# A convolution block stack on one core: softmax and norms spread over calendar ticks, block loads on GpSimd's queue, an inner product between two others

## The chip, the cores and the metric

The kernel runs on one core of a Trainium2 chip. The metric is the time of one execution in microseconds (us); lower is better. Three executions of the kernel before took 2953.84, 2951.65 and 2955.03 us. One more execution was taken with the hardware profiler; all profile lines here are from it.

## What is computed

The input x has 32 images of 14 x 14 positions and 512 channels, in float32. Two layers follow, each added to its input:

```python
x = x + L0(_gn(x))          # 18 blocks of gelu(x @ w[i] + b[i])
x = x + grouped_conv3x3(_gn(x), W)   # 32 groups

def L0(x):
    anchors = []
    for i in range(18):
        nx = gelu(x @ block_w[i] + block_b[i])
        if i in (11, 14, 17):                       # targets
            h = gelu(mean(nx, (1, 2)) @ fc1_w[t] + fc1_b[t])
            gates = softmax((h @ fc2_w[t] + fc2_b[t]).reshape(-1, 3, 512), axis=1)
            nx = nx + gammas[t] * sum_a(gates[:, a] * anchors[a])
        x = nx
        if i in (1, 4, 9):
            anchors.append(x)
    return x
```

`_gn` is a group norm over 32 groups of 16 channels without weights.

## The kernel before

**Tiles and pairs.** Two images (392 positions) make a tile, two tiles a pair; there are eight pairs, 0 to 7. Channels lie on the partitions. One *block* is one layer i of one pair p, written (p,i) here: a 512x512 weight matrix times 784 columns. The list `steps` gives the order of the blocks: pair 0's layers 0 to 11, and then, for each p, the first twelve layers of pair p+1 woven with the last six of pair p, three at a time. The blocks are numbered 0 to 144 in this order; block 141 is a gap that only carries other work.

**A block** (`block`, L538) multiplies 2x2 partitioned matrices with seven products in place of eight, with sums of weights (`s`, stored once in DRAM as `skeep`) and differences of activations (`t`). One of the seven is split once more in the same way (`Inner`, L495); its four parts are 128x196 matmuls between the 128x392 matmuls of the others, with weights `u` (kept in `ukeep`) and right sides `v`. PSUM accumulators are called x, y and z, two banks each. The first product, x, is copied by ScalarE to y (`save`, L599); the second product then adds to y, and a gelu (L576, for target layers L583) makes the first quarter of the output. The last quarter's gelu comes near the end of the block; the next block's y needs it.

A block *starts ahead* when `ahead(k)` (L387) is true: its first product is then an inner product whose parts were already run inside the block before. It is false for pair 0, for layer 0, for layers right behind a target and for (6,16): 40 blocks of 144. These begin with x (written at L613), the copies to y, then y (L617), then `inner.part(0)` of z.

**The calendar.** All other work is put on ticks, seven to a block, and `run(tick)` calls what stands there at seven places of the block's text. Ticks only fix the order in which instructions are written to the engines' queues; each engine then runs its queue in order and waits where it must. `ROOM` says how many us VectorE ("dve") and ScalarE ("act") have free in each tick of a block, and `put` (L130) takes the first tick with room. VectorE's room is 2.1, 0.8, 2.2, 2.6, 0.5, 0, 0 for ticks 0 to 6.

**The work that the change touches.**

- `plan_start` (L357) brings in a pair while an earlier one is computed. `copy_in` (L263) copies x to the DRAM tensor `xcol`. `load_blocks` (L270) loads one of eight parts: four DMAs `xb` of 32 partitions x 12 x 32 floats (48 KB in pieces of 128 bytes), and for every second part four DMAs `xr` of 8 KB. They go to SyncE's (SP's) queue, which also issues the weights (L404 to L409), `s` (L427) and `u` (L450). Three buffers take the parts; `turn_blocks` (L284) transposes one on VectorE in 32x32 squares, and the part three places on is loaded into its buffer. Then come statistics, `scales_mean` and `scales_rstd` (group sums on TensorE, small VectorE operations, a power on GpSimd), `scales_newton` and `norm_in`.
- Behind a target layer, `plan_head` (L841) puts `gate_hidden` (L717) and `gate_logits` (L733, TensorE) and `gate_softmax` (L743) on ticks of the following blocks. `gate_softmax` is VectorE, then ScalarE's tanh (L763), then VectorE again. `plan_gates` then puts `gate_part` (VectorE), `gate_last` (ScalarE, tile gq) and `gate_add`.
- The functions with `yield` are written so that each engine's share is a step; `whole` runs all steps at once, in one tick.
- GpSimd's (POOL's) queue holds the powers and 32 accumulating DMAs of `keep_base` (L784), `o<-xkeep`.

Behind the last block, `drain` lists the remaining tasks in an order of its own. The change leaves it alone.

Of the kernel before, what the change touches and what calls it, by code (L numbers as in the profile page):

```python
# [20 lines left out]
def kernel(  # L21
# [20 lines left out]
    nc = tc.nc  # L42
# [4 lines left out]
    NH = NCK // 2  # L47
    NI = 2
    N = NI * HW
    NT = B // NI  # L50
    NPAIR = NT // 2
# [36 lines left out]
    def whole(parts):  # L88

        for _ in parts:  # L90
            pass
# [8 lines left out]
    for p in range(NPAIR - 1):  # L100
        q = p + 1
        if q < NPAIR - 1:
            parts = [(q, 0, 3), (p, 12, 15), (q, 3, 6), (p, 15, 18), (q, 6, 12)]
# [17 lines left out]
    def at(tick, fn, *args):  # L121
        calendar[tick].append((fn, args))

    def room(e, tick):
        return left[e].get(tick, ROOM[e][tick % NP7] if tick < tend else TAIL[e])

    def hold(e, tick, us):
        left[e][tick] = room(e, tick) - us

    def put(first, need, fn, *args):  # L130

        tick = first
        while any(room(e, tick) < us for e, us in need.items()):
            tick += 1
        for e, us in need.items():
            left[e][tick] = room(e, tick) - us
        at(tick, fn, *args)
        return tick

    def run(tick):  # L140
        for fn, args in calendar.pop(tick, ()):
            fn(*args)


    ident = const.tile([P, P], F32, name="ident")
    make_identity(nc, ident)
# [67 lines left out]
    def scales_mean(d, lo=0, hi=NR):  # L214
        ps = group_sums(f"mps_{d['name']}_{lo}", d["st"][:, lo:hi, 1::3], hi - lo)
        yield
        st, mean, dv = d["st"][:, lo:hi], d["mr"][:, 0, lo:hi], d["dv"][:, lo:hi]
        nc.vector.tensor_scalar(mean, ps, 0.5, None, ALU.mult)
        nc.vector.tensor_tensor(
            dv, st[:, :, 1::3], mean.unsqueeze(2).to_broadcast([P, hi - lo, 2]), ALU.subtract  # L220
        )
        nc.vector.tensor_mul(dv, dv, dv)
        nc.vector.scalar_tensor_tensor(dv, dv, HW / 2.0, st[:, :, 2::3], ALU.mult, ALU.add)

    def scales_rstd(d, lo=0, hi=NR):

        ps = group_sums(f"vps_{d['name']}_{lo}", d["dv"][:, lo:hi], hi - lo)
        yield
        ve = d["ve"][:, lo:hi]
        nc.vector.tensor_scalar(ve, ps, 1.0 / HW, 1e-5, ALU.mult, ALU.add)  # L230
        yield
        nc.gpsimd.tensor_tensor(d["y"][:, lo:hi], ve, mhalf[:, lo:hi], ALU.pow)
# [10 lines left out]
    def scales_newton(d, lo=0, hi=NR, times=1):  # L243
        ve, y, e, mr = d["ve"][:, lo:hi], d["y"][:, lo:hi], d["e"][:, lo:hi], d["mr"]
        for i in range(times):
            nc.vector.tensor_mul(e, y, y)
            nc.vector.scalar_tensor_tensor(e, e, -0.5, ve, ALU.mult, ALU.mult)
            o = y if i < times - 1 else mr[:, 1, lo:hi]
            nc.vector.scalar_tensor_tensor(o, e, 1.5, y, ALU.add, ALU.mult)
        nc.vector.scalar_tensor_tensor(  # L250
            mr[:, 2, lo:hi], mr[:, 0, lo:hi], -1.0, mr[:, 1, lo:hi], ALU.mult, ALU.mult
        )
# [5 lines left out]
    TB = 32  # L258
# [11 lines left out]
    def load_blocks(t, c):  # L270
        d = starts.setdefault(t, {"xin": {}})
        cols = xcol[t // 2][t % 2 * N : (t % 2 + 1) * N].rearrange("n (k q i) -> q n k i", k=NCK, i=TB)
        xs = d["xin"][c] = inpool.tile([P, NTB, TB], F32, tag="xin", name=f"xb_{t}_{c}")
        for q in range(P // TB):
            nc.sync.dma_start(
                xs[q * TB : (q + 1) * TB],
                cols[q, : NTB * TB, c].rearrange("(n j) i -> j n i", j=TB),
            )
        if c % NH == 0:
            xr = d["xr", c // NH] = inpool.tile([P, NH, TB], F32, tag="xr", name=f"xr_{t}_{c}", bufs=2)  # L280
            for q in range(P // TB):
                nc.sync.dma_start(xr[q * TB : (q + 1) * TB], cols[q, N - TB :, c : c + NH])

    def turn_blocks(t, c):  # L284
        d = starts[t]
# [16 lines left out]
    pst = {}  # L302
# [54 lines left out]
    def plan_start(p):  # L357

        t0 = NP7 * at_step[p, 0]
        parts = [(2 * p + n, c) for n in range(2) for c in range(NCK)]  # L360
        NIN = 3
        a = t0 - LEAD
        at(a - 30, copy_in, p)
        turned = []
        b = 0
        for j, (t, c) in enumerate(parts):
            at(t0 - LEAD - 6 if j < NIN else turned[j - NIN], load_blocks, t, c)
            turned.append(put(max(a, turned[j - NIN] + 4 if j >= NIN else 0), {"dve": 0.45 + c % NH * 0.15}, turn_blocks, t, c))
            a = turned[j]
        for j, (t, c) in enumerate(parts):  # L370
            b = max(b, put(turned[j // NH * NH + NH - 1], {"dve": 0.7}, stats_in, t, c))
        b = put(b + 1, {"dve": 0.8}, lambda: whole(scales_mean(pst[p])))
        b = put(b + 1, {"dve": 0.2}, lambda: whole(scales_rstd(pst[p])))
        b = put(b + 2, {"dve": 0.8}, lambda: scales_newton(pst[p]))
        e = b
        for c in range(NCK):
            for n in range(2):
                e = max(e, put(b, {"dve": 0.8}, norm_in, p, c, (n,)))
        b = e

        assert b < t0 - 2
        at(t0 - 3, take_start, p)
# [4 lines left out]
    def ahead(k):  # L387


        p, i = steps[k]  # L390
        if (p, i) == (NPAIR - 2, TARGETS[1] + 2):
            return False
        return p > 0 and i not in (GAP, 0) and i - 1 not in TARGETS
# [144 lines left out]
    def block(k):  # L538
# [17 lines left out]
        def part(acc, d, lhsT, rhs, first=False, kks=range(NH)):  # L556
            for kk in kks:
                nc.tensor.matmul(  # L558
                    acc[d][:, :N], lhsT=lhsT[:, kk, d * P : (d + 1) * P],
                    rhs=rhs[:, kk, :], start=first and kk == 0, stop=kk == NH - 1,  # L560
                    skip_group_check=True,
                )
# [5 lines left out]
        def gelu(half, n, srcs, ds=range(NH)):  # L568
            if 0 in ds:
                dst[half][n] = quarter(f"o{half}{n}_{name}")  # L570
            o = dst[half][n]
            for d in ds:
                c = half * NH + d
                r = i * NCK + c
                if pooled is None:
                    nc.scalar.activation(  # L576
                        o[:, d, :], srcs[d], AF.Gelu_apprx_tanh, bias=bias[:, r : r + 1]
                    )
                else:
                    for b in range(NI):  # L580
                        sl = slice(b * HW, (b + 1) * HW)
                        m = n * NI + b
                        nc.scalar.activation(  # L583
                            o[:, d, sl], srcs[d][:, sl], AF.Gelu_apprx_tanh,
                            bias=bias[:, r : r + 1], accum_out=pooled[:, c, m : m + 1],
                        )
# [4 lines left out]
        def flat(acc):  # L591
            return [b[:, :N] for b in acc]
# [17 lines left out]
        else:  # L610
            X, Y = bank("x"), bank("y")
            for d in range(NH):
                part(X, d, w["a11"], q[0][0], True)  # L613
                save(Y, X, (d,))
        for kk in range(NH):
            for d in range(NH):
                part(Y, d, w["a12"], q[1][0], kks=(kk,))  # L617
        gelu(0, 0, flat(Y))
        Z = bank("z")
        inner = Inner(Z, s[0], w["u0"], t[0], t["v"], f"z{name}")  # L620
        inner.part(0)
        run(tick)
        c2 = temps(2)
        part(X, 0, s[1], t[1])
# [216 lines left out]
    def plan_head(p, i):  # L841

        k = at_step[p, i]
        t1 = NP7 * (k + 1)
        name = f"{p}_{i}"
        ti = TARGETS.index(i)
        box = boxes[p, i] = {}
        hn = [(h, n) for h in range(2) for n in range(2)]
        if i == NB - 1:
            for h, n in hn:  # L850
                a = max(boxes[p, TARGETS[-2]]["base"].values()) + 1
                assert put(a, {"act": 1.0}, keep_base, p, h, n) < t1 - NP7
        if k == len(steps) - 1:
            for (h, n), a in (((0, 0), 2), ((1, 1), 5), ((0, 1), 6)):
                at(NP7 * k + a, gate_base, p, i, h, n)
            return
        if p == 0:
            at(t1 + 1, gate_differences, k, ti)
        at(t1 + 1, lambda: whole(gate_hidden(k, ti, name, box)))
        box["base"] = {(h, n): put(t1, {"dve": 1.0}, gate_base, p, i, h, n) for h, n in hn}  # L860
        a = t1 + 2
        while room("dve", a) < 1.75:
            a += 1
        at(a, gate_logits, k, name, box)
        return put(a, {"dve": 1.75}, lambda: whole(gate_softmax(ti, name, box)))

    def plan_gates(p, t, a, chunks):

# [617 lines left out]


    NGAP = 6
    LEAD = 47
    for k in range(len(steps)):  # L1490
        p, i = steps[k]
        if i == GAP:
# [41 lines left out]
    b = NP7  # L1534
# [46 lines left out]
```

## Time and profile before

| | |
|---|---|
| median of three executions | 2953.84 us |
| profiled execution, its own time | 2947.32 us |
| its span, first to last instruction | 2945.6 us |
| TensorE (PE) busy | 2864.8 us, 97% |
| VectorE (DVE) busy | 2116.1 us, 72% |
| ScalarE (ACT) busy | 1630.1 us, 55% |
| GpSimd (POOL) busy | 79.1 us, 3% |
| DMA, mean | 172 GB/s |
| granted TensorE clock | 0.993 |

In the profile's lines, a group or a timeline row gives engine, line of the kernel, operation, output<-inputs with buffer numbers left out, and shapes. In a timeline row the first number is the start and the second the length, both in us, and the bracket at the end says how long the engine stood idle before it and who ended that. A float32 matmul shows as two records, so a product of four matmuls is "x8". "SPq" is the issuing of DMAs by SyncE; its length is the time of issue, not of the transfer. A line of the waits view reads: who waited <- for whom: us in total, times, longest. A busy TensorE is not a TensorE at its peak, since the ends of its pipelined matmuls are modelled.

### The profile page before, as it was taken

Reading aid. Unit: us, or ns where it says so; the run is one execution under the profiler, and the core shown is the slowest. Engines: PE = TensorE matmul, PEld = TensorE weight load, DVE = VectorE, ACT = ScalarE, POOL = GpSimd, SP = SyncE. Lnnn points to the kernel's source line nnn. Section 1 sums busy time; section 2 is a strip of 40 time slices with the busy share of each in tenths; the row PEclk is TensorE's granted clock in tenths of the full one; section 3 lists DMA queues with packets and bytes.
Section 4 is the critical chain, followed back from the end, with each engine's and each line's share of the span. In section 5 each row is a group of like instructions: output and inputs, shape, how many; then the busy total and the mean of one; then the engine's idle time right before and its main releaser. Section 6 shows DMA issues by size and latency. Waiting matters only on the chain.

```text
span 2945.6 us, 36255 instructions
## 1 busy us (share of the span) xinstructions
PE 2864.8 (97%) x11169; PEld 1960.5 (67%) x11169; DVE 2116.1 (72%) x4576; ACT 1630.1 (55%) x4281; POOL 79.1 (3%) x59
## 2 busy tenths in 40 slices
PE   9999999999999999999999999999999999999977
PEld 5666666666666666667666666666766676666666
DVE  6888887877778565875768756687567865766765
ACT  4445555566555665655556555565555555655551
POOL 0000000000000000000000000000000000000000
PEclk9999999999999999999999999999999999999999
DMA  6644566646564566647566465654766655453676
GB/s 205 180 163 158 172 191 174 183 139 195 163 183 143 162 185 172 187 135 209 170 188 187 142 185 168 189 165 148 203 177 184 175 151 155 143 161 125 180 212 160
DMA packets 528882, 505.69 MB, mean 172 GB/s; under 512 B 246883, under 2 KB 370610, under 8 KB 528690
## 3 DMA queue, kind: packets, MB, share of 16 engines
q1 hardware_dynamic: 513194, 485.30, 55.1%
q0 software_dynamic: 4608, 12.85, 2.5%
q10 hardware_dynamic: 10888, 5.22, 0.7%
q8 instruction: 91, 1.49, 0.2%
q14 instruction: 101, 0.83, 0.1%
HBM read 415.56 MB, written 98.93 MB: 175 GB/s over the span
## 4 chain that ended last, share of the span: by engine, by line
PE 84%; DVE 5%; ACT 5%; DMA 3%; SPq 1%; issue 1%; POOL 0%; ACTq 0%; DVEq 0%; POOLq 0%
PE x L558 36%; PE y L558 13%; PE z L507 11%; PE z L558 11%; PE x L507 7%; PE cps L1099 4%; ACT o L576 2%; PE lps L738 1%; ACT y L599 1%; DVE c L603 1%; ACT gq L823 1%; DMA x<-x2d 1%; PE hps L721 1%; DMA w<-ukeep 1%; DMA s<-skeep 1%
## 5 line engine op out<-in xcount | busy, mean ns | idle before, releaser
L558 PE MATMUL x<-t,s 128*128 128x392 f32 x2304 | 856.8, 494 | 5.0 <-DMA s<-skeep 2.9
L558 PEld LDWEIGHTS x<-t,s 128*128 128x128 f32 x2304 | 422.5, 190 | 167.3 <-DVE v_x L473 3.6
L558 PE MATMUL y<-o,w 128*128 128x392 f32 x1088 | 391.5, 500 | 23.3 <-ACT o L576 20.2
L558 PE MATMUL x<-t,w 128*128 128x392 f32 x1152 | 403.0, 492 | 0.0
L558 PE MATMUL z<-o,s 128*128 128x392 f32 x1088 | 398.0, 494 | 0.0
L603 DVE TENSOR_TENSOR c<-x,c 128x392 f32<-128x392 f32 x288 | 163.1, 566 | 277.6 <-ACT c L599 256.7
L576 ACT ACTIVATE o<-c,bias 128x392 f32<-128x392 f32 x480 | 282.9, 618 | 135.2 <-DVE c L603 134.6
L558 PEld LDWEIGHTS y<-o,w 128*128 128x128 f32 x1088 | 200.0, 189 | 201.4 <-ACT o L576 61.1
L599 ACT COPY c<-x 128x392 f32<-128x392 f32 x288 | 139.8, 485 | 323.5 <-PE x L558 323.5
L558 PEld LDWEIGHTS x<-t,w 128*128 128x128 f32 x1152 | 216.2, 190 | 130.8
L603 DVE TENSOR_TENSOR c<-z,c 128x392 f32<-128x392 f32 x288 | 157.8, 561 | 163.9 <-PE z L558 163.9
L491 DVE TENSOR_TENSOR t<-o,o 128x784 f32<-128x784 f32 x272 | 263.6, 969 | 6.5 <-ACT o L576 6.5
L558 PEld LDWEIGHTS z<-o,s 128*128 128x128 f32 x1088 | 200.8, 190 | 97.1 <-ACT c L599 0.5
L491 DVE TENSOR_TENSOR t<-o,t 128x784 f32<-128x784 f32 x272 | 263.1, 967 | 0.0
L576 ACT ACTIVATE o<-y,bias 128x392 f32<-128x392 f32 x240 | 140.8, 587 | 145.5 <-PE y L558 137.0
L507 PE MATMUL z<-v,u 128*128 128x196 f32 x864 | 214.0, 329 | 1.0 <-PE y L558 0.9
L507 PE MATMUL x<-v_x,w 128*128 128x196 f32 x832 | 193.7, 335 | 9.6 <-DMA w<-ukeep 8.9
L507 PEld LDWEIGHTS z<-v,u 128*128 128x128 f32 x864 | 156.9, 190 | 42.1 <-PE y L558 1.5
L532 DVE TENSOR_TENSOR z<-z,v 128x392 f32<-128x392 f32 x144 | 82.2, 570 | 139.3 <-ACT z L528 139.1
L507 PEld LDWEIGHTS x<-v_x,w 128*128 128x128 f32 x832 | 141.7, 190 | 48.1 <-issue 9.8
L576 ACT ACTIVATE o<-x,bias 128x392 f32<-128x392 f32 x240 | 135.5, 582 | 38.0 <-PE x L558 37.5
L599 ACT COPY y<-x 128x392 f32<-128x392 f32 x288 | 126.2, 461 | 54.1 <-PE x L558 54.0
(152 smaller groups left out, 3951.9 us busy)
## 6 DMA issues: line engine op xcount, KB each, us to landing
s<-skeep SPq DMA_DIRECT2D x504, 256.0 KB
w<-in_L_conv_block_w_dram SPq DMA_DIRECT2D x126, 512.0 KB
w<-in_L_conv_block_w_dram SPq DMA_DIRECT2D x126, 256.0 KB
u<-ukeep SPq DMA_DIRECT2D x126, 256.0 KB
w<-ukeep SPq DMA_DIRECT2D x104, 256.0 KB
x2d<-xc SPq DMA_DIRECT2D x116, 224.0 KB
x<-x2d SPq DMA_DIRECT2D x104, 224.0 KB
w<-in_L_conv_block_w_dram SPq DMA_DIRECT2D x18, 1024.0 KB
```

Of the source, the lines that this page charges most:

```text
L491: nc.vector.tensor_tensor(t[j], i0, i1, ALU.subtract)
L507: nc.tensor.matmul(self.corner(d, n), lhsT=lhsT, rhs=rhs, start=first, stop=True, skip_group_check=True,)
L532: nc.vector.tensor_tensor(both, both, self.f.unsqueeze(1).to_broadcast([P, 2, HW]), ALU.add)
L558: nc.tensor.matmul(acc[d][:, :N], lhsT=lhsT[:, kk, d * P : (d + 1) * P], rhs=rhs[:, kk, :], start=first and kk == 0, stop=kk == NH - 1, sk ...
L576: nc.scalar.activation(o[:, d, :], srcs[d], AF.Gelu_apprx_tanh, bias=bias[:, r : r + 1])
L599: nc.scalar.copy(cs[d][:, :N], acc[d][:, :N])
L603: nc.vector.tensor_tensor(cs[d], acc[d][:, :N], cs[d], ALU.add)
L721: nc.tensor.matmul(hps[:, :NB4], lhsT=w1[:, kk, :], rhs=box["pooled"][:, kk, :], start=(kk == 0), stop=(kk == NCK - 1),)
L738: nc.tensor.matmul(lps[:, m * NB4 : (m + 1) * NB4], lhsT=w2[:, (m - NCK) * P : (m - NCK + 1) * P], rhs=h, start=True, stop=True,)
L823: nc.scalar.activation(q[:, d, sl], anc[p][NA - 1][h][n][:, d, sl], AF.Identity, scale=gt[:, NA - 2, j : j + 1],)
L1099: nc.tensor.matmul(pv[:, :, lo:hi], lhsT=bw[:, g, dy], rhs=xv[:, :, lo + dy - 1 : hi + dy - 1], start=g == 0 and j == 0, stop=j == 2, skip ...
```

## The change

Four edits. (1) In a block that does not start ahead, `inner.part(0)` of z is written between the first product and y's; y's matmuls then go bank by bank. (2) `apart` runs the steps of a function on ticks of their own. The softmax of pairs 1 to 5 takes three ticks b, b+1, b+2, with b behind the tick of the logits and 1.5 us of room at b+2. (3) The input norm's two group sums take their steps on separate ticks. (4) `load_blocks` issues on GpSimd's queue, 336 DMAs in all. `LEAD` goes from 47 to 50, so a pair's load begins three ticks earlier.

```diff
+    def apart(fn, *ticks):
+        parts = []
+        def go():
+            if not parts:
+                parts.append(fn())
+            next(parts[0], None)
+        for tick in ticks:
+            at(tick, go)
...
-            nc.sync.dma_start(
+            nc.gpsimd.dma_start(
                 xs[q * TB : (q + 1) * TB],
                 cols[q, : NTB * TB, c].rearrange("(n j) i -> j n i", j=TB),
             )
...
-                nc.sync.dma_start(xr[q * TB : (q + 1) * TB], cols[q, N - TB :, c : c + NH])
+                nc.gpsimd.dma_start(xr[q * TB : (q + 1) * TB], cols[q, N - TB :, c : c + NH])
...
-        b = put(b + 1, {"dve": 0.8}, lambda: whole(scales_mean(pst[p])))
-        b = put(b + 1, {"dve": 0.2}, lambda: whole(scales_rstd(pst[p])))
-        b = put(b + 2, {"dve": 0.8}, lambda: scales_newton(pst[p]))
+        b += 1
+        e = put(b + 1, {"dve": 0.8}, lambda: None)
+        apart(lambda: scales_mean(pst[p]), b, e)
+        apart(lambda: scales_rstd(pst[p]), e + 1, e + 2, e + 2)
+        b = put(e + 4, {"dve": 0.8}, lambda: scales_newton(pst[p]))
...
-        for kk in range(NH):
-            for d in range(NH):
-                part(Y, d, w["a12"], q[1][0], kks=(kk,))
-        gelu(0, 0, flat(Y))
+        if ahead(k):
+            for kk in range(NH):
+                for d in range(NH):
+                    part(Y, d, w["a12"], q[1][0], kks=(kk,))
+            gelu(0, 0, flat(Y))
         Z = bank("z")
         inner = Inner(Z, s[0], w["u0"], t[0], t["v"], f"z{name}")
         inner.part(0)
+        if not ahead(k):
+            product(Y, w["a12"], q[1][0])
+            gelu(0, 0, flat(Y))
         run(tick)
...
-        return put(a, {"dve": 1.75}, lambda: whole(gate_softmax(ti, name, box)))
+        if p in (0, NPAIR - 2, NPAIR - 1):
+            return put(a, {"dve": 1.75}, lambda: whole(gate_softmax(ti, name, box)))
+        b = a + 1
+        while room("dve", b + 2) < 1.5:
+            b += 1
+        hold("dve", b, 0.7)
+        hold("dve", b + 2, 1.5)
+        apart(lambda: gate_softmax(ti, name, box), b, b + 1, b + 2)
+        return b + 2
...
-    LEAD = 47
+    LEAD = 50
```

## The prediction

> **What bounds the kernel.** The page's first part says that TensorE is busy for nearly the whole span, so only its waits can be won.
>
> ```profile
> PE 2864.8 (97%) x11169; PEld 1960.5 (67%) x11169; DVE 2116.1 (72%) x4576; ACT 1630.1 (55%) x4281; POOL 79.1 (3%) x59
> ```
>
> The second view is the list of who waited for whom, PE alone (us in total, times, longest):
>
> ```profile
> PE y L558 <- ACT o L576: 20.2, 41, 1.2
> ...
> PE x L507 <- DMA w<-ukeep: 8.9, 5, 2.7
> ...
> PE y L558 <- ACT y L599: 3.0, 8, 1.5
> PE x L558 <- DMA s<-skeep: 2.9, 3, 1.4
> ```
>
> These sums leave out what hides in the pipeline, so I took start-to-start spacings of the matmul records from the trace: 329 ns behind a 128x392, 166 ns behind a 128x196 when nothing waits; the excess is wait. That gives 134 us, of which start and drain hold some 46 and the change barely touches them. The rest: 45.5 us ahead of y (12.5 in the 40 blocks that do not start ahead, 33.0 in the 104 that do), about 20 for weights that came late, the rest small. Blocks that wait for nothing are 17.85 us apart.
>
> The third view is the timeline of the second block of pair 0:
>
> ```profile
> 37.97 2.80 PE L558 MATMUL x<-o,w 128*128 128x392 f32 x8
> ...
> 39.48 0.47 ACT L599 COPY y<-x 128x392 f32<-128x392 f32 x1 [0.73 <-PE x L558]
> ...
> 40.60 3.02 PE L558 MATMUL y<-o,w 128*128 128x392 f32 x8
> 40.85 0.47 ACT L599 COPY y<-x 128x392 f32<-128x392 f32 x1 [0.90 <-PE x L558]
> ...
> 43.46 0.49 PE L507 MATMUL z<-v,u 128*128 128x196 f32 x2
> ```
>
> y's second bank is copied until 41.32, while TensorE wants it two matmuls (0.66 us) after 40.60: y takes 2.86 us to the next start instead of 2.63, 0.22 lost.
>
> The fourth is the timeline around a gate's softmax, pair 2's in block (3,0):
>
> ```profile
> 941.16 1.84 PE L738 MATMUL lps<-h,w 128*128 128x4 f32 x16
> ...
> 943.05 0.19 DVE L749 TENSOR_TENSOR lg<-lps,bias 128x32 f32<-128x32 f32 x1 [1.72 <-PE lps L738]
> ...
> 945.48 0.25 DVE L774 SCALAR_TENSOR_TENSOR g<-ex,gam,ssum 128x32 f32<-128x32 f32 x1
> ...
> 946.82 1.03 DVE L603 TENSOR_TENSOR c<-z,c 128x392 f32<-128x392 f32 x2
> ...
> 948.45 0.79 ACT L823 ACTIVATE gq<-o,g 128x196 f32<-128x196 f32 x2
> ...
> 949.94 1.05 ACT L576 ACTIVATE o<-x,bias 128x392 f32<-128x392 f32 x2
> ...
> 950.57 2.90 PE L558 MATMUL y<-o,w 128*128 128x392 f32 x8 [1.20 <-ACT o L576]
> ```
>
> VectorE stands 1.72 us for the logits of its own tick, works on the softmax to 945.7, ScalarE then puts gq before the last gelu, and the next y is late.
>
> The fifth is SP's queue near 450 us:
>
> ```profile
> 446.30 2.04 SPq L275 DMA_DIRECT2D xb<-xcol  x4
> 448.38 2.08 SPq L282 DMA_DIRECT2D xr<-xcol  x4
> 450.51 4.79 SPq L275 DMA_DIRECT2D xb<-xcol  x8
> ...
> 459.56 0.59 SPq L408 DMA_DIRECT2D w<-ukeep  x1
> ```
>
> Eleven us of block loads stand ahead of the weights; a second batch follows at 461.83.
>
> **The change, part by part.**
>
> *Inner part between the products* (40 blocks not started ahead). No instruction is added. Two 128x196 matmuls (four records, 0.66 us) go between x and y, which covers the 0.22 us wait; v's last add ended at 40.16, before x ends at 40.60, so the new first operand is there. On ScalarE two Z copies (0.31 + 0.33) now precede the gelu of y, which waits for y anyway (idle 1.68 before it). Of the 12.5 us, block (6,16) alone has 1.77, where ScalarE is full of gq; it keeps 1.1. Gain 11.4. If v were late the cover would be gone and the 0.22 would stay.
>
> *Softmax on three ticks* (pairs 1 to 5, three gates each; pairs 0, 6 and 7 keep it whole). In the changed order the logits stay at tick 3, VectorE's first part goes to tick 5, tanh to tick 6, the rest to tick 0 of the next block, and gq leaves tick 4. The five waits like the one above (1.47 each by spacing, after blocks (q,0), q = 2 to 6) and the ten after (q,3) and (q,6) (0.75 each) are 7.35 + 7.5. I take 14.5. The first part (0.64 us) now precedes three 0.97 us adds; the first of them had 2.2 us to spare, so that is free; without this cover it is 15 times 0.64. Next late is the block behind, whose y waits 0.56 for a gq at tick 4 that is still there.
>
> *Norms on ticks of their own.* PE never waited for a group sum of pairs 1 to 7's input norms; VectorE stood 8.0 us for eight (mr_a from mps_a), off the path. I put 0; a gain is excluded by PE's list, a loss needs pair 1's last norm (now tick 79, pair 1 starts at 84) late. The power on POOL (2.9 us) is due 18 ticks after the last loads, so queueing behind them costs nothing.
>
> *Block loads to POOL's queue.* 224 xb (384 pieces of 128 B each) and 112 xr (64 pieces) leave SP. The six places where they stand ahead of weights and skeep loads (blocks 23, 41, 59, 77, 95, 113 and those behind) hold 18.2 us of excess. In four of these the order now has eight output stores (7.11 us of SP in block 77); stores without block loads behind blocks 68, 70 and 106 gave no wait. I take 15.5.
>
> The Trainium skill, "DMA: Bandwidth & Descriptors", section "Issuing engines are not separate DMA queues", says that issuing from another engine saves only the sequencer's time, usually small beside the transfer. By it this gain would be near 0. The rows above speak against it here: the weights were issued 8 us late because of issue alone.
>
> What POOL pays is not in the trace. The nearest row is the accumulating load, 128 pieces:
>
> ```profile
> L788 POOL DMA_DIRECT2D o<-xkeep x32: 844/874/1047, 372.9 to 2769.4; - x32
> ...
> 2175.01 1.73 POOL L788 DMA_DIRECT2D o<-xkeep  x2 [3.06 <-ACT o L787]
> ```
>
> Back to back they take 0.84 us. One xb costs c: at least 0.84 (all fixed), 2.5 if all goes by pieces (3 times 0.84), 3.1 if also stretched as the longest row is (1047 over 844). I take 1.7, the middle of the first two, since SP's own rows (xb 0.47 median for 384 pieces, xkeep 0.38 for 128) hardly grow with pieces; xr 0.7.
>
> Where it matters: the first three blocks of a pair wait on POOL only for the copy of x and the base loads, which end some 40 us before their turn (410 against 451). The next three wait for buffers that the first turns free, and the last of them lands 11c + 4 x 0.7 + 3 us later (landing 3, an estimate below the 4.7 of 392 KB). VectorE turns them 19.3 us later in pair 1 (one block of 18.6 and a turn of 0.57), 27.7 us later in pairs 3 to 7 (ten ticks). Behind a late turn on VectorE stand the c adds and pre-adds, so TensorE stops after about 2 us of slack (VectorE's idle 1.72 and 2.14 there). At c = 1.7 the sum is 24.5: pair 1 loses 3, the others 0. At 0.84 nothing is lost; at 2.5, 12 + 2.4 (pair 1's last group, 7c) + 5 x 3.6 = 32; at 3.1, 19 + 7 + 5 x 10 = 76.
>
> **Sum.** -11.4 - 14.5 - 15.5 + 3 = -38.4 us. Against the profiled execution's 2947.32 (span 2945.6) that is 2909; against the median 2953.84, which lies 6.5 above that execution, 2915. The median is the forecast.
>
> **Rivals.**
>
> *Issue on POOL between 2.1 and 2.6 us.* 8 to 40 us come back as stalls at the second turns. For it: POOL's only row is for fewer pieces. Against: SP's rows. About 2935 in the middle.
>
> *SP was not the cause.* The late weights stem from full DMA engines: four skeep loads took 7.70 us of issue at 711 us with no block loads near. Then the 15.5 is nothing and the result 2931. This is what the skill's rule above would give.
>
> *ScalarE's work only moves.* No gq is removed; y waits elsewhere. Only 4 of the 14.5 are won: 2926.
>
> *Slower: the block loads hold VectorE.* Place: second turns of pairs 1 and 3 to 7. From c = 2.6 the stalls (41 us) eat the gains; at 3.1 the result is 2953.84 - 41.4 + 76 = 2988. For it: the 1047 ns issue ran beside small VectorE operations. Against: the nine back-to-back issues are all 0.84 beside two-input VectorE adds. The Trainium skill, "SBUF — State Buffer", section "SBUF: two separate sides", has a box by which VectorE's two-port operations keep GpSimd from writing descriptors; it names 620 ns growing to 3100. The trace agrees only in that issues never fell below 844.
>
> That a part does nothing is the norms, counted as 0.
>
> **Chances.** Forecast as summed 0.56 (2905 to 2926); POOL at 2.1 to 2.6, 0.16, of which 0.05 lies within 0.2%; SP not the cause 0.10; work only moves 0.10; slower 0.08. 0.2% (5.9 us) is about what a measurement can tell from no change. Faster 0.87, same 0.05, slower 0.08. The low end takes all of 12.5, 14.85 and 18.2 with no stall (2908), less the 3 us by which the runs shown scatter: 2905; the high end reaches into POOL's case and leaves out its dear part and the slower one: 2938.
>
> **What would show it.** Right: y's 0.22 gone from pair 0 (pitch near 18.13); y after (q,0), (q,3), (q,6) without wait for pairs 1 to 5; no w<-ukeep or s<-skeep waits in blocks 23 to 114; POOL's xb at 1.7 us or less and no idle of VectorE ahead of L305's transposes. Wrong: transposes waiting for xb, or y waits as before with another releaser.

## The result

The changed kernel takes 2922.24 us (median of four executions, 2916.88 to 2926.05) where the kernel before takes 2952.74 on the same chip. The ratio is 0.9894, 95% interval 0.9874 to 0.9915: 30.5 us less. The forecast was 38.4 less, 2915, with a range of 2905 to 2938. The profiled execution took 2918.94 us (span 2916.6, against 2945.6 before).

The page's engines and its count of DMA packets:

```profile
PE 2855.6 (98%) x11169; PEld 1968.9 (68%) x11169; DVE 2115.2 (73%) x4576; ACT 1632.9 (56%) x4281; POOL 276.3 (9%) x395
...
DMA packets 441073, 505.67 MB, mean 173 GB/s; under 512 B 153699, under 2 KB 279218, under 8 KB 440882
```

No engine has other work than before but POOL, whose 79 us became 276 for 336 more instructions. The packets fell by 87,800 (528,882 before).

The list of who waited for whom, PE:

```profile
PE y L572 <- ACT o L590: 8.7, 26, 0.5
PE x L521 <- DMA w<-ukeep: 4.3, 5, 1.5
PE z L521 <- issue: 3.7, 1, 3.7
...
PE vps_b L221 <- DVE dv_b L235: 2.1, 7, 1.0
...
PE z L521 <- DVE u L473: 1.4, 1, 1.4
...
PE y L572 <- ACT y L613: 0.8, 1, 0.8
```

y's wait for the gelu fell from 20.2 to 8.7 us, y's wait for its copy from 3.0 to 0.8. The other lines tell of the costs: two waits of z that were not there (3.7 and 1.4), a group sum that waits for VectorE (2.1, from 0.3), and weights from ukeep that are still late, 4.3 in place of 8.9.

The excess of the start-to-start spacings, the measure of the prediction, fell from 132 (the prediction's count gave 134) to 103.5 us in these two profiled executions (A: blocks that start ahead, N: the others):

| place of the excess (us) | before | after |
|---|---|---|
| y, A | 33.0 | 17.5 |
| y, N | 12.5 | 2.8 |
| z's 128x196, N | 1.5 | 6.2 |
| other products; late weights are about 20 of it before, 6 after | 38.0 | 25.1 |
| output norm's sum, ahead of the drain | 0 | 2.9 |
| start and drain | 47.1 | 49.0 |

The timeline of pair 0's third block shows the new order:

```profile
60.15 0.47 ACT L613 COPY y<-x 128x392 f32<-128x392 f32 x1 [0.65 <-PE x L572]
...
60.31 0.36 DVE L487 TENSOR_TENSOR v<-v,t 128x196 f32<-128x196 f32 x1
...
60.43 0.57 PE L521 MATMUL z<-v,u 128*128 128x196 f32 x2 [0.37 <-DVE v L487]
...
61.16 2.80 PE L572 MATMUL y<-o,w 128*128 128x392 f32 x8
```

The cover works: y's second bank is copied until 60.62, before y begins at 61.16. Most blocks of pair 0, 18.35 us apart before, are now 18.12 apart, where the prediction had said 18.13. But v is not always there. Here z waits 0.37 us for it, because VectorE made four sums of weights (L473) first.

The timeline of the softmax behind block (2,0), where y had waited 1.47:

```profile
601.91 2.80 PE L572 MATMUL y<-o,w 128*128 128x392 f32 x8
...
602.66 0.17 DVE L767 TENSOR_TENSOR lg<-lps,bias 128x32 f32<-128x32 f32 x1
```

VectorE no longer waits for the logits, whose matmuls ended 7 us ago (at 595.7), and y has no bracket.

The worst place of z is block 142, (7,15), which stands behind the gap:

```profile
2739.23 2.80 PE L572 MATMUL x<-o,w 128*128 128x392 f32 x8
...
2740.05 2.76 DVE L815 TENSOR_TENSOR o<-o,o 128x784 f32<-128x784 f32 x3
...
2744.24 1.00 DVE L505 TENSOR_TENSOR t<-o,o 128x784 f32<-128x784 f32 x1
2745.28 0.36 DVE L487 TENSOR_TENSOR v<-t 128x196 f32<-128x196 f32 x1
...
2745.74 0.57 PE L521 MATMUL z<-v,u 128*128 128x196 f32 x2 [3.72 <-issue]
...
2746.48 4.49 PE L572 MATMUL y<-o,w 128*128 128x392 f32 x8
```

VectorE is still at the gap's work, starts the block's first t 5 us after x has begun, and z stands 3.7 us for v. The bracket says "issue"; the v row above it says who was late. Behind the wait, y takes 4.49 us in place of 2.80: its matmuls start 0.65 us apart, not 0.33, while the trace's granted clock is 0.5 (2746.5 to 2749.9). So y loses 1.7 us more without a bracket.

POOL's price, from the group of L287:

```profile
L287 POOL DMA_DIRECT2D xb<-xcol x224: 615/615/967, 46.3 to 2224.0; - x112
```

615 ns for a load of 384 pieces, under the 844 that the prediction had as its lowest case. No transpose of VectorE waits for an xb.

### The profile page after: what moved, and what is told of

It is laid out like the page before. It is cut to its first block, busy times and chain, and to the rows that moved or that the text cites. A ratio compares the mean times of both kernels' runs of the same rounds, so it can differ in the third digit from the quotient of the medians.

```text
span 2916.6 us, 36340 instructions
## 1 busy us (share of the span) xinstructions
PE 2855.6 (98%) x11169; PEld 1968.9 (68%) x11169; DVE 2115.2 (73%) x4576; ACT 1632.9 (56%) x4281; POOL 276.3 (9%) x395
## 3 DMA queue, kind: packets, MB, share of 16 engines
q8 instruction: 90, 1.47, 0.2%
## 4 chain that ended last, share of the span: by engine, by line
PE 88%; DVE 3%; ACT 3%; DMA 3%; SPq 1%; issue 1%; POOL 0%; DVEq 0%; ACTq 0%; POOLq 0%
PE x L572 38%; PE y L572 13%; PE z L572 12%; PE z L521 11%; PE x L521 8%; PE cps L1125 4%; PE lps L756 1%; ACT o L590 1%; DMA w<-ukeep 1%; DMA x<-x2d 1%; DVE c L617 1%; ACT gq L841 1%; ACT y L613 1%; PE hps L739 1%; DMA w<-in_L_conv_block_w_dram 0%
## 5 line engine op out<-in xcount | busy, mean ns | idle before, releaser
L572 PE MATMUL y<-o,w 128*128 128x392 f32 x1088 | 385.4, 497 | 9.8 <-ACT o L590 8.7
L287 POOL DMA_DIRECT2D xb<-xcol x224 | 138.6, 634 | 401.0 <-DVE xt L305 254.8
L806 POOL DMA_DIRECT2D o<-xkeep x32 | 28.0, 879 | 1510.8 <-ACT o L805 805.1
```

Source lines behind the costliest of these rows:

```text
L287: nc.gpsimd.dma_start(xs[q * TB : (q + 1) * TB], cols[q, : NTB * TB, c].rearrange("(n j) i -> j n i", j=TB),)
L572: nc.tensor.matmul(acc[d][:, :N], lhsT=lhsT[:, kk, d * P : (d + 1) * P], rhs=rhs[:, kk, :], start=first and kk == 0, stop=kk == NH - 1, sk ...
```

## Experiments

The theory after this result: the softmax and the loads gave what was forecast; the inner part gave only 5 us, since its cover goes where v is late; and two things that had no price took something back: the place of copy_in (moved by LEAD) and that of the output norm. Rivals: the sums of the trace are chance of one execution; late weights have nothing to do with issue; and POOL's second turns were never in danger.

### One part taken back

Four kernels, each the changed one with one part as before, on one chip (the kernel before there: 2951.34).

**The product y ahead of z again, in all blocks.**

```diff
-        if ahead(k):
-            for kk in range(NH):
-                for d in range(NH):
-                    part(Y, d, w["a12"], q[1][0], kks=(kk,))
-            gelu(0, 0, flat(Y))
+        for kk in range(NH):
+            for d in range(NH):
+                part(Y, d, w["a12"], q[1][0], kks=(kk,))
+        gelu(0, 0, flat(Y))
...
-        if not ahead(k):
-            product(Y, w["a12"], q[1][0])
-            gelu(0, 0, flat(Y))
```

> The changed kernel with the order x, y, inner part in every block, as before. By the prediction's size of this edit the time is 11.4 us above the changed kernel (2922), 2934. By the profile after, the edit won 10.9 us in the ordinary blocks but lost 5.9 in blocks 0, 2 and 142, where the inner part's operands come late: then the time is only 5 us above, 2927, the 0.22 us waits of y are back in some 38 blocks, and block 142 has its 3.95 + 1.69 us back to 1.2 + 0.2.

Measured: 2924.14, ratio 0.9914 (0.99 to 0.9929), an interval that overlaps the changed kernel's. By spacing, y in N blocks has 12.15 again and z's 128x196 there 1.52 in place of 6.2: the edit is worth 4.7 us of wait, 9.3 of y less 4.7 of z. The medians are 2 us apart, so the time alone does not show a gain. From before to after, the same two rows of the table give 5.0: the ordinary blocks and (6,16) won 10.6, nearly what was forecast, and blocks 142, 0 and 2 lost 5.6.

**The block loads on SP again.**

```diff
-            nc.gpsimd.dma_start(
+            nc.sync.dma_start(
                 xs[q * TB : (q + 1) * TB],
...
-                nc.gpsimd.dma_start(xr[q * TB : (q + 1) * TB], cols[q, N - TB :, c : c + NH])
+                nc.sync.dma_start(xr[q * TB : (q + 1) * TB], cols[q, N - TB :, c : c + NH])
```

> The changed kernel with the block loads on SyncE's queue again. If SyncE's issue time made the weights late: 14 us above the changed kernel, 2936, with waits for w<-ukeep and s<-skeep of 2 to 5 us back in five or six of the blocks 23 to 114. If the DMA engines' load was the cause and issuing from another engine saves little: no difference, 2922, and no such waits beyond those of the changed kernel.

Measured: 2930.91, 0.993 (0.9917 to 0.9943), 9 to 11 us over the changed kernel, where 14 was expected. By spacing, waits are back in blocks 78 (6.4 us), 97 (1.6) and 59 (0.5), and block 114 has 7.5 in place of 1.5. Blocks 23, 24, 41, 42, 95 and 96 still have none. So with the loads on SP, other parts of the change suffice there; the likely one is that the loads stand three ticks earlier, but no run sets LEAD back alone.

**The softmax whole again, in one tick.**

```diff
-        if p in (0, NPAIR - 2, NPAIR - 1):
+        if True:
```

> The changed kernel with the softmax of all pairs in one tick. If its waits on VectorE make y late: about 15 us above the changed kernel, 2937, with 1.47 us ahead of y behind blocks (q,0) and 0.75 behind (q,3) and (q,6) for q = 2 to 6. If ScalarE's gq work sets it and only moves: 4 us above, 2926.

Measured: 2929.68, 0.9927 (0.9914 to 0.9939). The y excess of A blocks goes from 17.5 to 28.8, with 0.75 in each of blocks (q,1), (q,4) and (q,7), q = 2 to 6. So the softmax's ticks are worth 11.3 us of y, fifteen times 0.75; by the ratios the time is 10 us longer. The output norm's wait also rises, from 2.9 to 6.9, and the weights of blocks 37 and 55 are on time, as the longer blocks would let them be.

The 1.47 that was expected in blocks (q,1) did not come back. In the kernel before, the output norm's `scales_newton` stood in the same place of block (3,0), behind the softmax and ahead of the c adds:

```profile
946.10 0.17 DVE L246 TENSOR_TENSOR e_b<-y_b 128x16 f32<-128x16 f32 x1
...
946.72 0.17 DVE L250 SCALAR_TENSOR_TENSOR mr_b<-mr_b 128x16 f32<-128x16 f32 x1
```

Its four operations take 0.79 us there. In the changed kernel, and in this one, the output norm's plan has moved and they come earlier, in the first third or so of the block. Blocks (2,1) to (7,1) each won the other 0.72 by that, 4.3 us in all; in (7,1), whose softmax stays whole in every kernel, it is seen alone (1.47 to 0.75). With the block loads alone on POOL it stays 1.47. The move is there with each single part taken back, so LEAD, or two of the other parts, made it.

**The input norm's sums whole again.**

```diff
-        apart(lambda: scales_mean(pst[p]), b, e)
-        apart(lambda: scales_rstd(pst[p]), e + 1, e + 2, e + 2)
-        b = put(e + 4, {"dve": 0.8}, lambda: scales_newton(pst[p]))
+        b = put(b + 1, {"dve": 0.8}, lambda: whole(scales_mean(pst[p])))
+        b = put(b + 1, {"dve": 0.2}, lambda: whole(scales_rstd(pst[p])))
+        b = put(b + 2, {"dve": 0.8}, lambda: scales_newton(pst[p]))
```

> The changed kernel with the input norm's group sums in one tick each, as before. By the prediction this part is worth 0: 2922 within 2 us. A rival: the freed room of VectorE moved the output norm to ticks 5 and 6, where TensorE waits for it (vps_b 3.8 us in the profile after, 0.5 before); with the norms whole these waits go and the time is 3 us lower, 2919.

Measured: 2920.05, 0.9897 (0.9883 to 0.991). No difference in the time, as forecast. By spacing two waits are gone with it, 1.1 us each in blocks 29 (the output norm's sum) and 34 (below), but late weights are more in this execution and hide that.

### The block loads alone, on the kernel before

```diff
     def load_blocks(t, c):
...
-            nc.sync.dma_start(
+            nc.gpsimd.dma_start(
                 xs[q * TB : (q + 1) * TB],
...
-                nc.sync.dma_start(xr[q * TB : (q + 1) * TB], cols[q, N - TB :, c : c + NH])
+                nc.gpsimd.dma_start(xr[q * TB : (q + 1) * TB], cols[q, N - TB :, c : c + NH])
```

> The kernel before with the block loads on GpSimd's queue and nothing else changed. By the prediction -15.5 us, and no stall since the issue costs 0.6 us: a ratio of 0.995 (14.8 us). Waits of blocks 23/24, 41/42, 59/60, 77/78, 95/96 and 113/114 (18 us of spacing) go. Rival (the rule that moving issue between queues saves little): within 3 us of the kernel before. Taking the loads back to SP in the changed kernel cost about 10 us; if that is what they are worth everywhere, it is -10 here.

Measured: 2931.04, 0.9925 (0.9908 to 0.9943), 20 us less than the 2950.98 of before; 16.4 by spacing. PE's waits for weights from ukeep, five for 8.9 us before, are one in its list, and those for skeep are gone:

```profile
PE x L507 <- DMA w<-ukeep: 1.6, 1, 1.6
```

The 18.2 us of excess in blocks 23/24, 41/42, 59/60, 77/78, 95/96 and 113/114 are all gone. That the weights stood behind the batch in SP's queue, and not in full DMA engines, can be seen in the kernel before itself. The DMA view of the 35 us from 440 us, in 40 slices of 0.875 us, busy tenths of the 16 engines:

```profile
DMA  0000007996611466624139989989997564116679
```

The first batch of block loads was issued from 446.3 to 457.2. From 448 us on (the tenth to the twenty-first digit) the DMA engines were busy for only 1 to 6 tenths. The weights w<-ukeep could have gone at about 452, as they did at 452.44 with the loads on POOL; they went at 459.56. On POOL's queue the loads also become other packets: in the trace's DMA records each piece of 128 bytes is a packet of its own on SP's queue (93,184 of them), and on POOL's 24 pieces of an xb go as one of 3072 bytes. Whether SP's batch was slow by its issues or by its packets wasn't tried apart.

The Trainium skill, "DMA: Bandwidth & Descriptors", section "Issuing engines are not separate DMA queues", has it that another issuing engine saves only the sequencer's time, usually small beside the transfer. That the gain is small does not hold here: the 336 DMAs are worth 10 us (loads back) to 20 (loads alone), and their issues took SP 185 us in the kernel before, 11 of them ahead of this block's weights.

### POOL made dear

Where is the point at which the block loads would hold VectorE? Each xb cut into four; in a second kernel the 4 is an 8.

```diff
-            nc.gpsimd.dma_start(
-                xs[q * TB : (q + 1) * TB],
-                cols[q, : NTB * TB, c].rearrange("(n j) i -> j n i", j=TB),
-            )
+            for r in range(4):
+                lo, hi = r * TB // 4, (r + 1) * TB // 4
+                nc.gpsimd.dma_start(
+                    xs[q * TB + lo : q * TB + hi],
+                    cols[q, : NTB * TB, c].rearrange("(n j) i -> j n i", j=TB)[lo:hi],
+                )
```

> The changed kernel with each xb load cut into four of 96 pieces. If an issue has a fixed part of some 0.55 us (xr, 64 pieces, takes 0.53), the load of a part of 32 columns costs GpSimd about 2.2 us in place of 0.615. By the prediction's formula the second turns are then late by 9 us in pair 1 and by nothing to 1 us in pairs 3 to 7: 9 to 13 us slower than the changed kernel, and VectorE waits ahead of the transposes at L305. If the price goes by pieces, four quarters cost 0.62 and the time is unchanged. Rival to the formula: the buffers come free earlier than worked out, and even 2.2 us of issue costs nothing.

> The changed kernel with each xb load cut into eight of 48 pieces, so that GpSimd pays about 4.2 to 4.4 us for what was 0.615 (if the fixed part is 0.53 to 0.55). By the prediction's formula the late turns cost 33 us in pair 1's first group, 15 in its last, and 24 in each of pairs 3 to 7, about 170 us in all; the rival that ended slower is then shown as a mechanism, with only its price wrong. If the time stays within 15 us of the changed kernel the formula's slack was wrong as well.

Measured: 2973.85 for quarters (ratio 1.007, 1.0051 to 1.0089), 3410.31 for eighths (1.1548, 1.1528 to 1.1568). The group of the quarters' issues:

```profile
L289 POOL DMA_DIRECT2D xb<-xcol x896: 577/578/922, 46.2 to 2300.9; - x180
```

VectorE now waits for xb, 48.4 us in seven waits. An issue takes 578 ns for 96 pieces, 603 for 48, 615 for 384, 533 for the 64 of xr: in these runs the price is per DMA and hardly depends on its pieces. The quarters' timeline at pair 3's second turns:

```profile
811.05 1.03 DVE L307 STREAM_TRANSPOSE xt<-xb 128x384 f32<-128x384 f32 x2
811.91 11.52 POOL L289 DMA_DIRECT2D xb<-xcol  x20 [1.86 <-DVE xt L307]
...
833.41 0.58 POOL L289 DMA_DIRECT2D xb<-xcol  x1 [1.73 <-DMA xb<-xcol]
...
838.05 0.57 DVE L307 STREAM_TRANSPOSE xt<-xb 128x384 f32<-128x384 f32 x1
...
848.24 0.58 DVE L307 STREAM_TRANSPOSE xt<-xb 128x384 f32<-128x384 f32 x1 [9.62 <-DMA xb<-xcol]
...
853.10 3.64 PE L574 MATMUL y<-o,w 128*128 128x392 f32 x5 [6.90 <-ACT o L592]
```

The first turns free the buffers at 811; the third part is wanted at 838.6, 27 us later (the prediction had 27.7); it lands at 848; VectorE's c adds are behind it, and y is late by 6.9. Between the issues POOL also waits for its own earlier DMAs ("DMA xb<-xcol"), so that an xb of four quarters costs more than 4 x 0.578: 48 quarters took 32.5 us here (34.7 less 2.15 for xr), c = 2.7, and 2.45 in pair 1. The prediction's formula with these gives 11 x 2.45 + 5.8 - 21.3 = 11.4 for pair 1's first group, 1.7 for its last and 5 x (11 x 2.7 + 5.8 - 29.7) = 29 for pairs 3 to 7: 42 us. By spacing these places got 15.2, 5.2 and 30.4, together 51; the median lies 52 above the changed kernel's. So the expectation of 9 to 13 was wrong mainly by its c of 2.2. Of the 51, some 13 are no waits: as in block 142, the matmuls behind a long wait start 0.65 us apart for a while (the granted clock is 0.5 from 848.6 to 858.9 here), which the formula does not count. The waits themselves are 38. For the eighths, c = 5.0 in pair 1 gives 39.5, 19.5 and 155; these places got 46, 26 and 158, of which 11 are matmuls at the lower clock. The other 260 us are at later turns, which the formula does not count.

### Where the rest was lost: the place of copy_in

New waits stand in blocks 34, 37 and 55 (1.1, 1.8 and 1.5 us by spacing), with a fourth in 109 (0.5). Those of 37, 55 and 109 are for w<-ukeep. In 34 it is v_x that is late: VectorE had stood 3.1 us ahead of L1023, a part of the second layer's weights. SP's queue before block 37 in the changed kernel, and PE behind it:

```profile
711.24 3.43 SPq L277 DMA_DIRECT2D xcol<-in_x_dram  x4
...
715.31 0.88 SPq L422 DMA_DIRECT2D w<-ukeep  x1
...
724.17 0.57 PE L521 MATMUL x<-v_x,w 128*128 128x196 f32 x2 [1.46 <-DMA w<-ukeep]
```

copy_in (1.6 MB from DRAM to DRAM) stands at the tick LEAD + 30 ahead of a pair's start. With LEAD at 47 it stood behind a block's weights; three ticks earlier it stands ahead of them. (The expectations below say "three blocks"; it is three ticks.) Four kernels were run on one chip (before: 2949.37), the first being the changed kernel once more.

> The changed kernel once more, as the reference for the other three on the same chip: 2917 to 2926 us, excess of PE's spacing about 103 us. If the waits for w<-ukeep in blocks 34, 37, 55 and 109 are set by the order of the calendar they come back here with the same blocks (each 0.4 to 1.8 us); if they are chance of one execution they move.

Measured: 2921.55, 0.9895 (0.9879 to 0.991). The waits of the four blocks: 1.0, 0, 1.8 and 0.4. Three are in the same places as in the other profiled execution, so the places are set by the order; block 37's wait is not in every execution. Blocks 37, 55, 73, 91 and 109 are (q,4) for q = 2 to 6, one place in each pair's plan. Together they hold 3.9 us in the changed kernel's first profile, 2.4 here, 6.4 with y first and 9.0 with the norms whole. That fits the 7 to 9 us by which this kernel's executions differ.

```diff
-        at(a - 30, copy_in, p)
+        at(a - 27, copy_in, p)
```

> The changed kernel with copy_in back three blocks later, at the tick it had when LEAD was 47, so that its four DMAs (3.43 us of SP) no longer stand just ahead of the next block's weights. Theory: the w<-ukeep waits of blocks 34, 37, 55 and 109 (1.09, 1.76, 1.52 and 0.46) go and the time falls by 3 to 5 us. Rival (those weights come late for another reason, the transfer itself): the waits stay in these blocks, and the time is that of the changed kernel.

Measured: 2913.13 (2912.51 to 2913.82), 0.9868 (0.9854 to 0.9883): 8.4 us less than the changed kernel, where 3 to 5 was expected, and its executions lie 1.3 us apart. No (q,4) block waits any more. The two profiled executions are only 3.9 us apart, 2 of it in these blocks; the rest of the 8.4 would be such waits in the executions without a profile, which is not shown. Block 34's 1.06 stays, as its other cause would have it. So do block 114's late weights (1.5 to 1.8 us in the three profiles so far, none with the loads alone on POOL); their cause is open.

Is it SP's time, or the copy itself? The same four DMAs, at their tick, on POOL's queue:

```diff
     def copy_in(p):
         for b in range(NB4):
-            nc.sync.dma_start(
+            nc.gpsimd.dma_start(
```

> The changed kernel with copy_in's four DMAs on GpSimd's queue, at their tick. Theory (the weights of the next block are late because they stand behind these DMAs on SP, 3.43 us of issue): the waits for w<-ukeep in blocks 34, 37, 55 and 109 go as they did when copy_in stood three blocks later, and the time is about 2913 to 2915 where the changed kernel gives 2922. Rival (the copy's own transfer, 392 KB out and in for each of four, fills the DMA engines when the weights are to land): the waits stay, 2918 to 2926.

Measured: 2925.71 (2920.47 to 2933.17), on a chip whose kernel before takes 2950.98: 0.991 (0.9883 to 0.9937). The timeline at block 37:

```profile
712.01 2.42 POOL L277 DMA_DIRECT2D xcol<-in_x_dram  x4 [0.19 <-issue]
...
716.40 0.38 SPq L420 DMA_DIRECT2D w<-in_L_conv_block_w_dram  x1
716.84 0.70 SPq L422 DMA_DIRECT2D w<-ukeep  x1
...
727.01 0.57 PE L521 MATMUL x<-v_x,w 128*128 128x196 f32 x2 [1.73 <-DMA w<-ukeep]
```

SP had nothing left to issue from 713.8 on. The weights' buffer came free when the block's x ended, at 716.38, and SP issued them at once; they still came 10 us later, and block 37 waits 2.0 by spacing. Block 109 waits 2.2 and 73 0.4; 55 is on time in this execution. The theory that SP's issue was the cause falls. The rival holds: the copy's own transfer is in front. Its four DMAs landed from 720.0 to 724.0, and the DMA engines were busy for 8 tenths or more of every 0.6 us from 714 to 725. Moving the copy to another queue does nothing; putting it behind the weights does. Here the rule of the Trainium skill's section named above is right.

### The other two costs

y ahead of z also in blocks 0 and 142:

```diff
-        if ahead(k):
+        if ahead(k) or k == 0 or steps[k - 1][1] == GAP:
...
-        if not ahead(k):
+        if not (ahead(k) or k == 0 or steps[k - 1][1] == GAP):
```

> The changed kernel with y ahead of z also in block 0 and in block 142, the two starts-not-ahead blocks where v came late. Theory (cover lost only where v is late): block 142's z goes from 3.95 to about 1.2 us and its y from 1.69 to about 0.2, block 0's z from 1.64 to 0.35, so 5 us less than the changed kernel, some 2917 where that gives 2922. Rival (the 4 us at block 142 would be spent elsewhere in the last pair, since the drain's end is set by the end norm and the last products): the drain grows by as much and the time stays within 1 us of the changed kernel.

Measured: 2924.67, 0.9903 (0.9885 to 0.9921). The two blocks did what was expected (142: z from 4.5 to 1.2, y from 1.1 to 0.2; block 0: z to 0.35; the drain the same), but the profiled execution, at 2926.95, had 9 us more late weights in the five blocks (q,4), and the median shows no gain where 5 us was expected. Alone it is inconclusive: the copy's waits scatter more than it wins.

All three: y ahead of z in these two blocks, copy_in three ticks later, and, as the only new edit, the output norm kept off ticks 5 and 6:

```diff
         b = last + 1
+        while b % NP7 > 4:
+            b += 1
         for us, fn, step in (
```

> The changed kernel with y ahead of z in blocks 0 and 142, copy_in three blocks later, and the end norm kept off the last two ticks of a turn of seven. If the three costs are real and apart, 5 + 4 + 3 us come off: about 2910 to 2912 where the changed kernel gives 2922. If one of them only uncovers another wait, 2914 to 2918.

Measured: 2905.98 (2903.34 to 2907.19), 0.9842 (0.9825 to 0.9858): 15.6 us below the changed kernel and 7.2 below the one with copy_in alone; 2910 to 2912 was expected. By spacing, against the latter, block 142 went from 5.6 to 1.3, block 0's z from 1.1 to 0.35, and block 34's wait (1.06), which each of the other two edits alone had left, went too. Of the output norm's 2.9 us only block 29's 1.15 went; five blocks keep 0.36, so that cost was read half wrongly. The four make 7.2.

## Why the prediction was right or wrong

- **Inner part, -11.4: mechanism right, size wrong; 5.0 by spacing.** The term failed at "v's last add ended at 40.16, before x ends at 40.60, so the new first operand is there". That was read in one block and carried to all forty. The other blocks gave 10.6, and (6,16) kept 1.1 as forecast. Block 142 lost 4.3, since VectorE was 5 us behind with the gap's work, and 1.5 of that is y's matmuls at half the clock behind the wait; blocks 0 and 2 lost 1.3. The prediction had said that a late v takes the cover away, and priced that at the 0.22 of the block. What is lost is the lateness of v itself, since z used to come a product (2.6 us) later and now waits for it.
- **Softmax, -14.5: mechanism right, but a part of the gain is luck; 11.3.** A blocks won 15.5 of y: the five of 1.47 went to 0, the ten of 0.75 too, and (7,1) halved. Taken back alone the softmax is worth 11.3, fifteen times 0.75. The step that failed is that the whole 1.47 was put down to it: 0.72 of each was the output norm's Newton step behind it, which moved without being meant to. The 0.56 of the block behind stayed, as named. The rival "only 4 are won" falls; a small piece of it is seen, 0.31 us that went from (q,9) to (q,10) in pairs 2 to 6.
- **Norms, 0: right in the time** (two waits of 1.1 us by spacing went with the edit taken back).
- **Block loads, -15.5: right in cause and size when alone** (16.4 by spacing, 20 in the median), 13 in the changed kernel, because new late weights came. So the sign "no w<-ukeep waits in blocks 23 to 114" did not hold: 37, 55, 88, 109 and 114 still wait. "SP was not the cause" falls by the kernel with this part alone.
- **POOL's price, +3: wrong, 0.** c is 0.615, below the lowest bound of 0.84. That bound took the accumulating load for a floor; it is another kind of DMA, and nothing in the trace made it one. The two rivals that hang on c were right as mechanisms: with c raised, the stalls stand where they were said to stand, 51 us where the formula gives 42 with the measured c, and 230 where it gives 214. (By the same formula the 2.4 and 7 that the prediction has for pair 1's last group are 2.0 and 6.2; its totals hardly change.) The point from which the slower case decides, c = 2.6, stands: the quarters, at 2.45 to 2.7, are slower than the kernel before. It needed four times the price that POOL has.
- **Not in the sum: LEAD, up to 8.4 us.** Its three ticks were told as a part of the change and never priced. They move copy_in too, from behind a block's weights to ahead of them. With copy_in where it was, the time is 2913.13 on a chip with 2949.37 before, 36 less; the forecast's 38.4 then misses by two. The output norm's move was not seen either: 2.9 lost ahead of its sum on ticks 5 and 6, and the 4.3 won in the blocks (q,1).

By spacing, the two profiled executions are 28.6 us apart where the sum has 38.4. Of that difference the inner part is 6.4, the weights and other products 2.6, the output norm's sum 2.9, and start and drain 1.9; against it stand 3 of POOL and 1 of the y in A blocks. The time lies well inside the range in part because errors offset each other: the price of POOL that did not come, and the 4.3 us of the Newton step, which made up for a softmax that gave 3.2 less than forecast.

## What to carry to other kernels

When an operation is moved ahead in an engine's order, read its operand's lateness in every kind of block in which it is moved, the first, the one behind a gap and the one with extra work among them; the cover is worth 0.2 us a block, and one block where it is absent can cost 4, a part of it in slower matmuls behind the wait. When a constant moves a whole plan, list everything that hangs on it, its bulk transfers above all, and see which weights each passes. A bulk transfer that delayed another was not helped by another queue here; put it behind the one that is urgent.

## What was not expected of the hardware

A plain DMA of 384 pieces of 128 bytes took POOL 615 ns to issue, an accumulating one of 128 pieces 844; plain ones of 48 to 384 pieces took 533 to 615. Behind TensorE's long waits (3.7 us in block 142, 12.5 in the quarters' longest) the granted clock was 0.5 for some us, and matmuls started 0.65 us apart in place of 0.33: 1.7 us more in block 142, some 2 at most places of the quarters. The Trainium skill, "SBUF — State Buffer", section "SBUF: two separate sides", tells of VectorE keeping GpSimd from writing descriptors, with a DMA's 620 ns growing to 3100 beside a VectorE copy. Beside a VectorE that is busy 73% of the span, the longest of 224 issues took 967, so here the trace does not show it. Several xb in quick succession do make POOL wait for its own earlier DMAs, up to 2.4 us at a time with quarters.
